# A selective-scan kernel on one core: the scan's operands trade memories, and GpSimd forms du*B for five states of sixteen

## The chip, the core and the metric

The kernel runs on one core of a Trainium2 chip. Its engines are named as the profile names them: PE is TensorE (matmuls), DVE is VectorE, ACT is ScalarE, POOL is GpSimd, SP is SyncE, which only issues transfers. The metric is device time in microseconds (us) of one execution; lower is better. Three executions of the kernel before took 4989.82, 4993.41 and 4997.49 us, and the median, 4993.41 us, is the time that the change is measured against.

## What is computed

Two layers follow each other. The change touches the first alone, a state-space block on a 4 x 48 x 48 x 128 image batch. Each image is projected to 256 channels, convolved, and read as a sequence of 2304 places in K = 4 directions. Each direction has N = 16 states per channel. For every state the first-order recurrence below runs along the sequence, and the 16 states are summed with the weights C:

```python
def step(h, inp):
    dt_l, u_l, B_l, C_l = inp
    dA = jnp.exp(dt_l[..., None] * A)
    h = h * dA + (dt_l * u_l)[..., None] * B_l[:, :, None, :]
    y = jnp.einsum('bkdn,bkn->bkd', h, C_l)
    return (h, y)
h0 = jnp.zeros((B, K, d, N), x.dtype)
_, ys = lax.scan(step, h0, (dt_t, u_t, B_t, C_t))
```

Around it stand a normalisation of the input, a softplus that makes dt, a normalisation and a gate behind the sum of the directions, and an output projection. The second layer is a Fourier neural operator with attention; it reads the first layer's output and stays as it is.

## The kernel before, in words

**Tiles and steps.** 256 channels lie as NF = 2 halves of 128 partitions. A sequence of 2304 places is cut into chunks of LC = 480 places (line 33), the last with 384. Four images, four directions and five chunks make 80 chunks; each has 16 steps, one for a state, so that there are 1280 steps. A step works on both halves at once: 2 x 480 elements per partition.

**What one step does.** The function names are those of lines 502 to 580.
- `fetch` (line 502) has SP load the rows of C for two states at a time, spread over all partitions, into `cbc` (three buffers); for a state that POOL drives it loads the row of B into `bbc` (two buffers).
- `drive_pool` (line 512) takes a buffer of `db` (three buffers, SBUF). For states with i % 4 == 3 (`POOLS`, line 604) POOL writes du*B into it.
- `spread` (line 519) has PE spread the row of B over the partitions into `pb`, one PSUM bank, for the other twelve states; `drive_in` (line 531) has DVE multiply du by `pb` into `db`.
- `decay` (line 538) has ACT write exp(dt*A) for both halves into `da`, one of two PSUM tiles of two banks each (line 478), chosen by i % 2. The first half ends at column 510, column 511 holds a zero that was set once (line 480), and the second half begins at 512. A last small ACT copy puts the state that was carried from the chunk before into the one column of `db` between the halves.
- `scan` (line 547) has DVE run one scan over 961 columns, h = da*h + db. At the parting column da is zero and db is the carried state, so the second half starts from its own state. The result goes to `h` (four buffers, SBUF).
- `read_out` (line 556) has POOL multiply `h` by C into `hc` (four buffers); `carry_on` (line 561) has ACT save the two last columns for the next chunk; `sum_up` (line 566) has PE add `hc` up in PSUM; `put_away` (line 582) has ACT copy the sums out after the sixteenth step.

**The order of the work** is written by hand. `LAGS` (line 626) lists the stages with how many steps behind the newest each runs, and `advance` (line 632) calls them in that order once for each new step. So on each engine the instructions stand in exactly this order (`Ordered`, line 36), while the transfers that SP issues may be placed earlier by the compiler. At the end of each round `piece` (line 610) emits one piece of side work: projections of the next direction (`project`, line 400), the next image's front part (`front`, line 260), an earlier chunk's output part (`back`, line 421). Side work waits its turn in the list `later`.

**Limits around it.** dt and the rows of B live in a ring of seven chunks (line 71); `project` may work on a chunk only once `done[0] + RING - 1` has reached its number (line 405), and its last piece runs the softplus of all five chunks of a direction (line 408). At step 11 of a direction's last chunk the rest of that projection is drained at once (line 694), since POOL then needs the first dt (`drive`, line 412).

Of the kernel before, what the change touches and what calls it, by code (L numbers as in the profile page):

```python
# [10 lines left out]
F32 = mybir.dt.float32  # L11
BF16 = mybir.dt.bfloat16
AF = mybir.ActivationFunctionType
# [10 lines left out]
NF = D // 128  # L24
N = 16
R = 8
K = 4
NX = 112
BANK = 512
NH = 32  # L30

LC = 480
CHUNKS = [(s, min(LC, L - s)) for s in range(0, L, LC)]


# [18 lines left out]
def first_layer(ctx, tc, io, x1_dram, sp_dram, d_w, d_m):  # L54
# [9 lines left out]
    on = Ordered(tc)  # L64
    const = ctx.enter_context(tc.tile_pool(name="l0_const", bufs=1))
    small = ctx.enter_context(tc.tile_pool(name="l0_small", bufs=2))
    one = ctx.enter_context(tc.tile_pool(name="l0_one", bufs=1))
    two = ctx.enter_context(tc.tile_pool(name="l0_two", bufs=2))
    three = ctx.enter_context(tc.tile_pool(name="l0_three", bufs=3))
    four = ctx.enter_context(tc.tile_pool(name="l0_four", bufs=4))  # L70
    ring = ctx.enter_context(tc.tile_pool(name="l0_ring", bufs=7))
    ps_a = ctx.enter_context(tc.tile_pool(name="l0_psa", bufs=1, space=PSUM))
    ps_s = ctx.enter_context(tc.tile_pool(name="l0_pss", bufs=1, space=PSUM))
    ps_b = ctx.enter_context(tc.tile_pool(name="l0_psb", bufs=1, space=PSUM))
# [24 lines left out]

    w_xp = const.tile([128, K, NF, NX], F32, name="w_xp")  # L100
    on.gpsimd.memset(w_xp, 0.0)
    w_x = const.tile([128, K, NF, R + 2 * N], F32, name="w_x")
    for k in range(K):
        nc.sync.dma_start(w_x[:, k], io["x_proj_wT"][k].rearrange("(f p) c -> p f c", p=128))
    for o, c0, c1 in ((0, R, R + 2 * N), (32, 0, R), (64, R, R + N), (96, R, R + N)):
# [258 lines left out]
    def project_chunk(c, w_dt, xc):  # L364


        k, s, n = c.k, c.s, c.n
        src = at(xc, k, s, n)
        px = side(f"px{c.t}")
        for f in range(NF):  # L370
            on.tensor.matmul(
                like(px[0:NX, 0:n], k), w_xp[:, k, f], src[:, f], start=(f == 0), stop=(f == NF - 1)
            )
            yield
        xd = two.tile([32 + R, LC], F32, tag="xd", name=f"xd{c.t}")
        on.scalar.copy(xd[:, 0:n], px[0 : 32 + R, 0:n])
        c.cd = dram.tile([2 * N, LC], F32, tag="cd", name=f"cd{c.t}")
        nc.sync.dma_start(c.cd[:, 0:n], xd[0 : 2 * N, 0:n])

        c.bs = ring.tile([NX, LC], BF16, tag="bs", name=f"bs{c.t}")  # L380
        on.scalar.copy(c.bs[:, 0:n], px[0:NX, 0:n])
        for q in range(2):
            on.tensor.matmul(px[0:NX, 0:n], less[:, q], c.bs[:, 0:n], start=False, stop=True, skip_group_check=True)
            yield
            rows = slice(64 + 32 * q, NX)
            on.scalar.copy(c.bs[rows, 0:n], px[rows, 0:n])
        c.dt = ring.tile([128, NF, LC], F32, tag="dt", name=f"dt{c.t}")
        for f in range(NF):
            pd = side(f"pd{c.t}_{f}")
            on.tensor.matmul(  # L390
                pd[:, 0:n],
                w_dt[32 : 32 + R, f * 128 : (f + 1) * 128],
                xd[32 : 32 + R, 0:n],
                start=True,
                stop=True,
            )
            yield
            on.scalar.activation(c.dt[:, f, 0:n], pd[:, 0:n], AF.Identity, bias=b_dt[:, k, f : f + 1])
# [77 lines left out]


    das = [ps_a.tile([128, 2 * BANK], F32, name=f"da{j}") for j in range(2)]
    for da in das:
        on.vector.memset(da[:, BANK - 1 : BANK], 0.0)  # L480
    carries = [const.tile([128, N, NF], F32, name=f"carry{j}") for j in range(2)]

    def halves(ap, n):

        return ap[:, 0 : 2 * (n + 1)].rearrange("p (f n) -> p f n", f=NF)[:, :, 0:n]

    class Chunk:


        def __init__(self, b, k, s, n, first, final, number, im):  # L490
            self.b, self.k, self.s, self.n, self.number, self.im = b, k, s, n, number, im
            self.first, self.final, self.rev = first, final, int(k >= 2)
            self.ready = False
            self.t = f"{b}_{k}_{s}"

    class Step:


        def __init__(self, c, i):
            self.c, self.i = c, i  # L500

    def fetch(u):
        c, i, n = u.c, u.i, u.c.n
        if i % NQ == 0:
            c.cbc = three.tile([128, NQ, LC], F32, tag="cbc", name=f"cbc{c.t}_{i}")
            nc.sync.dma_start(c.cbc[:, :, 0:n], c.cd[N + i : N + i + NQ, 0:n].partition_broadcast(128))
        u.cbc = c.cbc[:, i % NQ : i % NQ + 1, 0:n]
        if i % 4 == POOLS:
            u.bbc = two.tile([128, 1, LC], F32, tag="bbc", name=f"bbc{c.t}_{i}")
            nc.sync.dma_start(u.bbc[:, :, 0:n], c.cd[i : i + 1, 0:n].partition_broadcast(128))  # L510

    def drive_pool(u):

        c, i, n = u.c, u.i, u.c.n
        u.db = three.tile([128, NF * (LC + 1)], F32, tag="db", name=f"db{c.t}_{i}")
        if i % 4 == POOLS:
            on.gpsimd.tensor_mul(halves(u.db, n), c.du[:, :, 0:n], u.bbc[:, :, 0:n].to_broadcast([128, NF, n]))

    def spread(u):

        c, i, n = u.c, u.i, u.c.n
        if i == N - 1:
            done[0] = c.number + 1
        if i % 4 == POOLS:
            return
        u.pb = ps_b.tile([128, 512], F32, tag="pb", name=f"pb{c.t}_{i}")
        on.tensor.matmul(
            u.pb[:, 0:n], pick[:, i : i + 1].to_broadcast([NX, 128]), c.bs[:, 0:n], start=True, stop=True
        )

    def drive_in(u):
        c, i, n = u.c, u.i, u.c.n
        if i % 4 != POOLS:
            on.vector.tensor_mul(
                halves(u.db, n), c.du[:, :, 0:n], u.pb[:, None, 0:n].to_broadcast([128, NF, n])
            )

    def decay(u):
        c, i, n = u.c, u.i, u.c.n
        u.da = das[i % 2]  # L540
        for f in range(NF):
            q = c.k * NF + f
            o = BANK if f else BANK - 1 - n
            on.scalar.activation(u.da[:, o : o + n], c.dt[:, f, 0:n], AF.Exp, scale=a_neg[:, q, i : i + 1])
        on.scalar.copy(u.db[:, n : n + 1], c.carry[:, i, 1 - c.rev : 2 - c.rev])

    def scan(u):
        c, i, n = u.c, u.i, u.c.n
        u.h = four.tile([128, NF * (LC + 1)], F32, tag="h", name=f"h{c.t}_{i}")
        m = 2 * n + 1  # L550
        ha, aa, ba = u.h[:, 0:m], u.da[:, BANK - 1 - n : BANK + n], u.db[:, 0:m]
        if c.rev:
            ha, aa, ba = ha[:, ::-1], aa[:, ::-1], ba[:, ::-1]
        on.vector.tensor_tensor_scan(ha, aa, ba, c.carry[:, i, c.rev : c.rev + 1], ALU.mult, ALU.add)
# [45 lines left out]


    ORDER = (0, 2, 1, 3)
    RING = 7
    POOLS = 3
    WAIT, FREE = object(), object()
    current = [None]
    done = [0]
# [13 lines left out]
    def drain(gen):  # L621
        while gen in later:
            piece()


    LAGS = (
        (0, fetch), (9, put_away), (2, drive_pool), (4, drive_in), (5, scan), (4, decay), (6, carry_on),
        (5, read_out), (3, spread), (8, sum_up),
    )
    window = deque([None] * 10, 10)  # L630

    def advance(u):
        window.appendleft(u)
        for lag, stage in LAGS:
            if window[lag] is not None:
                stage(window[lag])
        piece()
# [30 lines left out]
    for j, chunks in enumerate(directions):  # L668
# [9 lines left out]
        for m, c in enumerate(chunks):  # L678
            c.carry = carries[j % 2]
            for i in range(N):  # L680
# [6 lines left out]
                if i in (N // 2 + 3, N // 2 + 6):  # L687
# [5 lines left out]
                    elif nxt is not None:  # L693
                        drain(nxt)
                        drive(directions[j + 1][0], f)
                advance(Step(c, i))
                if not chunks[-1].ready and not j:
                    piece()
    for _ in range(len(window)):
# [1287 lines left out]
```

## Time and profile before

| What | Value |
|---|---|
| median of three executions | 4993.41 us (4989.82 to 4997.49) |
| profiled execution, first to last instruction (span) | 4987.4 us |
| DVE busy over the span | 4169.9 us (84%) |
| POOL busy over the span | 3992.7 us (80%) |
| PE, ACT busy over the span | 4176.6 us, 2964.0 us |
| first and last scan begin at | 76.8 us, 4176.0 us |
| DMA share of 16 engines, mean | 32.5% on SP's queue |

The profile describes one execution of its own, whose only time is its span: it leaves out what lies before the first and after the last instruction. The shortest of the three timed executions is 2.4 us longer than that span, the median 6.0 us. A row of the groups gives an engine, an operation, what is written and read, how often it runs, its total busy time and the mean of one, and then the engine's idle time just before it with what ended that idle time. Each row mixes shapes unless they are kept apart. A wait is put down to what came last, so the name behind the arrow is the last missing thing, not always the cause.

### The profile page before, as it was taken

The numbers are of one execution on the slowest core, as the hardware profiler recorded it, in microseconds if no ns is written. First come the engines' busy times: TensorE is split into PE (matmuls) and PEld (weight loads), VectorE is DVE, ScalarE is ACT, GpSimd is POOL, SyncE is SP. The second block draws the span as 40 slices with busy tenths as digits, with TensorE's granted clock in tenths as the row PEclk, the third lists the DMA queues.
The fourth block names the chain that finished last, engine by engine and source line by source line (L and its number), as shares of the span: only waits on it lengthen the run. The fifth ranks groups of instructions, "written<-read, shape, count | busy, mean of one in ns | idle before, by whom it ended". The sixth has DMA issues, their size and how long they took to land.

```text
span 4987.4 us, 44228 instructions
## 1 busy us (share of the span) xinstructions
PE 4176.6 (84%) x12444; PEld 1913.7 (38%) x12444; DVE 4169.9 (84%) x2901; ACT 2964.0 (59%) x6608; POOL 3992.7 (80%) x2188
## 2 busy tenths in 40 slices
PE   6888898888798998887989888877888786879876
PEld 3334433333343333333433333333333432445443
DVE  3599998989899989898999998888999985557636
ACT  3566566666666666766666676665767654323344
POOL 4589998989899989888999998888999985146631
PEclk9989999999899999998999999998999988989977
DMA  1223232323232333232323233233333322236636
GB/s 55 74 87 100 94 113 91 104 85 102 90 107 94 116 95 99 89 100 92 104 95 115 93 98 94 98 104 92 104 107 102 105 92 90 48 71 147 146 101 151
DMA packets 276388, 491.57 MB, mean 99 GB/s; under 512 B 105685, under 2 KB 189781, under 8 KB 275565
## 3 DMA queue, kind: packets, MB, share of 16 engines
q1 hardware_dynamic: 270560, 485.67, 32.5%
q10 hardware_dynamic: 5580, 3.08, 0.3%
q8 instruction: 98, 1.61, 0.1%
q14 instruction: 150, 1.22, 0.1%
HBM read 453.49 MB, written 35.38 MB: 98 GB/s over the span
## 4 chain that ended last, share of the span: by engine, by line
DVE 18%; PE 15%; issue 7%; ACT 7%; POOL 3%; DMA 2%; SPq 1%; DVEq 0%; POOLq 0%; ACTq 0%
DVE h L50 12%; PE yp L50 4%; ACT da L50 3%; DVE db L50 3%; PE acc L1404 2%; ACT L50 1%; PE sc L1267 1%; POOL v L1400 1%; POOL db L50 1%; PE pi_p L50 1%; DMA xrep<-dxt 1%; ACT dt L50 1%; POOL hc L50 1%; ACT ws L50 1%; PE px L50 1%
## 5 line engine op out<-in xcount | busy, mean ns | idle before, releaser
L50 POOL TENSOR_TENSOR hc<-h,cbc 128x960 f32<-128x960 f32 (+1 forms) x1280 | 2718.7, 2140 | 448.3 <-DVE h L50 335.8
L50 DVE TENSOR_TENSOR_SCAN h<-da,carry,db 128x961 f32<-128x961 f32 (+1 forms) x1280 | 2701.8, 2129 | 164.9 <-ACT carry L50 107.1
L50 ACT ACTIVATE da<-dt,a_neg 128x480 f32<-128x480 f32 (+1 forms) x2560 | 1666.6, 651 | 1176.6 <-DVE h L50 1130.8
L50 PE MATMUL yp<-hc,ident 128*128 128x480 f32 (+1 forms) x5120 | 2277.5, 572 | 17.7 <-POOL hc L50 17.4
L50 PEld LDWEIGHTS yp<-hc,ident 128*128 128x128 f32 x5120 | 1005.6, 198 | 1381.0 <-issue 1006.0
L50 DVE TENSOR_TENSOR db<-du,pb 128x960 f32<-128x960 f32 (+1 forms) x960 | 1063.8, 1108 | 233.2 <-PE pb L50 177.8
L50 POOL TENSOR_TENSOR db<-du,bbc 128x960 f32<-128x960 f32 (+1 forms) x320 | 688.9, 2153 | 17.2 <-DMA d_m<-in_wK 8.5
L50 PE MATMUL pb<-bs,pick 112*128 112x480 bf16 (+1 forms) x960 | 358.0, 373 | 351.9 <-DVE db L50 350.0
L50 PE MATMUL pc<-pad,cdiag 128*128 128x480 f32 (+1 forms) x630 | 284.1, 563 | 6.6 <-ACT pad L50 6.6
L1400 POOL TENSOR_TENSOR v<-grep,xrep 128x768 f32<-128x768 f32 x96 | 174.9, 1823 | 87.3 <-PE acc L1404 48.7
L50 ACT COPY db<-carry 128x1 f32<-128x1 f32 x1280 | 228.5, 178 | 19.5 <-POOL db L50 13.5
L1404 PE MATMUL acc<-v,attn_c 128*64 128x384 f32 x1152 | 211.5, 504 | 26.7 <-DVE v L1396 13.6
L50 POOL TENSOR_TENSOR du<-dt,xc 128x480 f32<-128x480 f32 (+1 forms) x160 | 204.9, 1281 | 34.0 <-ACT dt L50 34.0
L1396 DVE TENSOR_TENSOR v<-gp,xrep 128x1536 f32<-128x1536 f32 x96 | 168.0, 1756 | 74.4 <-PE acc L1404 46.4
L50 PE MATMUL px<-xc,w_xp 128*112 128x480 f32 (+1 forms) x320 | 214.0, 756 | 17.1 <-ACT xc L50 13.3
L50 PEld LDWEIGHTS <-pick 112*128 112x128 bf16 x960 | 97.7, 102 | 329.4 <-issue 306.1
L50 ACT ACT_TABLE_LOAD x148 | 189.9, 1283 | 50.3 <-DMA ws_M<-in_wM1s 26.7
L50 PE MATMUL pd<-xd,w_dt 8*128 8x480 f32 (+1 forms) x320 | 168.0, 605 | 40.0 <-ACT bs L50 24.5
L50 ACT COPY carry<-h 128x2 f32<-128x2 f32 x1024 | 194.4, 190 | 0.0
L50 PEld LDWEIGHTS pc<-pad,cdiag 128*128 128x128 f32 x630 | 122.1, 194 | 139.4 <-issue 114.6
L50 PE MATMUL yp<-y,ident 128*128 128x480 f32 (+1 forms) x240 | 166.3, 823 | 0.2
L1404 PEld LDWEIGHTS acc<-v,attn_c 128*64 128x64 f32 x1152 | 119.2, 139 | 108.5 <-issue 53.7
(366 smaller groups left out, 3102.2 us busy)
## 6 DMA issues: line engine op xcount, KB each, us to landing
cbc<-cd SPq DMA_DIRECT2D x512, 480.0 KB
bbc<-cd SPq DMA_DIRECT2D x256, 240.0 KB
cbc<-cd SPq DMA_DIRECT2D x128, 384.0 KB
xrep<-dxt SPq DMA_DIRECT2D x48, 576.0 KB
bbc<-cd SPq DMA_DIRECT2D x64, 192.0 KB
grep<-dgt SPq DMA_DIRECT2D x16, 576.0 KB
x<-in_xT SPq DMA_DIRECT2D x16, 288.0 KB
xr<-in_xT SPq DMA_DIRECT2D x16, 288.0 KB
```

Source lines behind the costliest of these rows:

```text
L50: return lambda *args, **kw: self._tc.keep_in_program_order(emit(*args, **kw))
L1267: nc.tensor.matmul(sc[64 * b : 64 * b + 64, g, 0 : 8 * T], qs[:, j, n, 2 * pair + b], f[b][:, 8 * g : 8 * g + 8], start=(jn == 0), stop=False,
L1396: nc.vector.tensor_mul(v, gp[:, None, :, 0:NC].to_broadcast([128, 2, 2, NC]), x[:, :, 0:2])
L1400: nc.gpsimd.tensor_mul(v3, r[:, 2:3].to_broadcast([128, 2, NC]), x[:, :, 2])
L1404: nc.tensor.matmul(acc[c][64 * b : 64 * b + 64, 0:NC], attn_c[:, 2 * pair + b, g, q], v[:, b, c] if c < 2 else v3[:, b], start=first, stop ...
```

## The change

The sixteen states get kinds by the string `KINDS`: eleven V (DVE forms du*B) and five P (POOL does, for i = 2, 5, 8, 11, 14; before there were four, i = 3, 7, 11, 15).
- **V states.** The decay no longer goes to PSUM but to one of three SBUF tiles, `ahead`, chosen by the running step number modulo 3, and ACT writes it one round earlier (lag 3 in place of 4). DVE now writes du*B into the PSUM tile `held`, which is what `da` was, and the scan reads decay from SBUF and du*B from PSUM.
- **P states** keep decay in PSUM (`held`) and du*B in SBUF (`db`, now two buffers), at lag 4 as before.
- **Two parting columns** in place of one: halves stand at columns 482 apart in `h` and `db`, scans run over 962 columns. `part` has ACT write them: for a V state the carried state into two columns of `held`; for a P state the carried state into `db`, and zeros into `held` where a V state used it last. All five P states of a chunk follow a V state on the same tile. The decay tiles' own zeros are set once.
- **Room.** The ring of dt and B rows goes from seven chunks to six; `xd` has one buffer in place of two; a start-up tile, `w_x`, shares the place of `y`.

```diff
@@ -30,6 +30,10 @@
 NH = 32
 LC = 480
+GAP = 2
+AHEAD = 3
+RING = 6
+KINDS = "VVPVVPVVPVVPVVPV"
 CHUNKS = [(s, min(LC, L - s)) for s in range(0, L, LC)]
@@ -68,7 +72,7 @@
     two = ctx.enter_context(tc.tile_pool(name="l0_two", bufs=2))
     three = ctx.enter_context(tc.tile_pool(name="l0_three", bufs=3))
     four = ctx.enter_context(tc.tile_pool(name="l0_four", bufs=4))
-    ring = ctx.enter_context(tc.tile_pool(name="l0_ring", bufs=7))
+    ring = ctx.enter_context(tc.tile_pool(name="l0_ring", bufs=RING))
     ps_a = ctx.enter_context(tc.tile_pool(name="l0_psa", bufs=1, space=PSUM))
     ps_s = ctx.enter_context(tc.tile_pool(name="l0_pss", bufs=1, space=PSUM))
     ps_b = ctx.enter_context(tc.tile_pool(name="l0_psb", bufs=1, space=PSUM))
@@ -99,7 +103,7 @@
     w_xp = const.tile([128, K, NF, NX], F32, name="w_xp")
     on.gpsimd.memset(w_xp, 0.0)
-    w_x = const.tile([128, K, NF, R + 2 * N], F32, name="w_x")
+    w_x = one.tile([128, K, NF, R + 2 * N], F32, tag="y", name="w_x")
     for k in range(K):
         nc.sync.dma_start(w_x[:, k], io["x_proj_wT"][k].rearrange("(f p) c -> p f c", p=128))
     for o, c0, c1 in ((0, R, R + 2 * N), (32, 0, R), (64, R, R + N), (96, R, R + N)):
@@ -372,7 +376,7 @@
                 like(px[0:NX, 0:n], k), w_xp[:, k, f], src[:, f], start=(f == 0), stop=(f == NF - 1)
             )
             yield
-        xd = two.tile([32 + R, LC], F32, tag="xd", name=f"xd{c.t}")
+        xd = one.tile([32 + R, LC], F32, tag="xd", name=f"xd{c.t}")
         on.scalar.copy(xd[:, 0:n], px[0 : 32 + R, 0:n])
         c.cd = dram.tile([2 * N, LC], F32, tag="cd", name=f"cd{c.t}")
         nc.sync.dma_start(c.cd[:, 0:n], xd[0 : 2 * N, 0:n])
@@ -476,13 +480,17 @@
     das = [ps_a.tile([128, 2 * BANK], F32, name=f"da{j}") for j in range(2)]
-    for da in das:
-        on.vector.memset(da[:, BANK - 1 : BANK], 0.0)
+    parted = [True, True]
+    zero = const.tile([128, GAP], F32, name="zero")
+    on.gpsimd.memset(zero, 0.0)
+    ahead = [const.tile([128, 2 * LC + GAP], F32, name=f"ahead{j}") for j in range(AHEAD)]
+    for t in ahead:
+        on.gpsimd.memset(t[:, LC : LC + GAP], 0.0)
     carries = [const.tile([128, N, NF], F32, name=f"carry{j}") for j in range(2)]
     def halves(ap, n):
-        return ap[:, 0 : 2 * (n + 1)].rearrange("p (f n) -> p f n", f=NF)[:, :, 0:n]
+        return ap[:, 0 : 2 * (n + GAP)].rearrange("p (f n) -> p f n", f=NF)[:, :, 0:n]
     class Chunk:
@@ -496,8 +504,9 @@
     class Step:
-        def __init__(self, c, i):
-            self.c, self.i = c, i
+        def __init__(self, c, i, g):
+            self.c, self.i, self.g, self.kind = c, i, g, KINDS[i]
+            self.held = das[i % 2]
     def fetch(u):
         c, i, n = u.c, u.i, u.c.n
@@ -505,15 +514,15 @@
             c.cbc = three.tile([128, NQ, LC], F32, tag="cbc", name=f"cbc{c.t}_{i}")
             nc.sync.dma_start(c.cbc[:, :, 0:n], c.cd[N + i : N + i + NQ, 0:n].partition_broadcast(128))
         u.cbc = c.cbc[:, i % NQ : i % NQ + 1, 0:n]
-        if i % 4 == POOLS:
+        if u.kind == "P":
             u.bbc = two.tile([128, 1, LC], F32, tag="bbc", name=f"bbc{c.t}_{i}")
             nc.sync.dma_start(u.bbc[:, :, 0:n], c.cd[i : i + 1, 0:n].partition_broadcast(128))
     def drive_pool(u):
-        c, i, n = u.c, u.i, u.c.n
-        u.db = three.tile([128, NF * (LC + 1)], F32, tag="db", name=f"db{c.t}_{i}")
-        if i % 4 == POOLS:
+        c, n = u.c, u.c.n
+        if u.kind == "P":
+            u.db = two.tile([128, NF * (LC + GAP)], F32, tag="db", name=f"db{c.t}_{u.i}")
             on.gpsimd.tensor_mul(halves(u.db, n), c.du[:, :, 0:n], u.bbc[:, :, 0:n].to_broadcast([128, NF, n]))
     def spread(u):
@@ -521,34 +530,60 @@
         c, i, n = u.c, u.i, u.c.n
         if i == N - 1:
             done[0] = c.number + 1
-        if i % 4 == POOLS:
+        if u.kind != "V":
             return
         u.pb = ps_b.tile([128, 512], F32, tag="pb", name=f"pb{c.t}_{i}")
         on.tensor.matmul(
             u.pb[:, 0:n], pick[:, i : i + 1].to_broadcast([NX, 128]), c.bs[:, 0:n], start=True, stop=True
         )
+    def half(ap, m, f, n):
+        o = m + GAP if f else m - n
+        return ap[:, o : o + n]
+    def whole(ap, m, n):
+        return ap[:, m - n : m + GAP + n]
+    IN_PS = BANK - GAP
     def drive_in(u):
+        c, n = u.c, u.c.n
+        if u.kind == "V":
+            on.vector.tensor_mul(
+                halves(u.held[:, IN_PS - n :], n), c.du[:, :, 0:n], u.pb[:, None, 0:n].to_broadcast([128, NF, n])
+            )
+    def decay(u, kind):
         c, i, n = u.c, u.i, u.c.n
-        if i % 4 != POOLS:
-            on.vector.tensor_mul(
-                halves(u.db, n), c.du[:, :, 0:n], u.pb[:, None, 0:n].to_broadcast([128, NF, n])
-            )
-    def decay(u):
-        c, i, n = u.c, u.i, u.c.n
-        u.da = das[i % 2]
+        if u.kind != kind:
+            return
+        u.da, m = (u.held, IN_PS) if kind == "P" else (ahead[u.g % AHEAD], LC)
         for f in range(NF):
             q = c.k * NF + f
-            o = BANK if f else BANK - 1 - n
-            on.scalar.activation(u.da[:, o : o + n], c.dt[:, f, 0:n], AF.Exp, scale=a_neg[:, q, i : i + 1])
-        on.scalar.copy(u.db[:, n : n + 1], c.carry[:, i, 1 - c.rev : 2 - c.rev])
+            on.scalar.activation(half(u.da, m, f, n), c.dt[:, f, 0:n], AF.Exp, scale=a_neg[:, q, i : i + 1])
+        u.da = whole(u.da, m, n)
+    def part(u):
+        c, i, n = u.c, u.i, u.c.n
+        start = c.carry[:, i, 1 - c.rev : 2 - c.rev].to_broadcast([128, GAP])
+        between = u.held[:, IN_PS:BANK]
+        if u.kind == "P":
+            if parted[i % 2]:
+                on.scalar.copy(between, zero)
+            on.scalar.copy(u.db[:, n : n + GAP], start)
+            u.db = u.db[:, 0 : 2 * n + GAP]
+        else:
+            on.scalar.copy(between, start)
+            u.db = whole(u.held, IN_PS, n)
+        parted[i % 2] = u.kind != "P"
     def scan(u):
         c, i, n = u.c, u.i, u.c.n
-        u.h = four.tile([128, NF * (LC + 1)], F32, tag="h", name=f"h{c.t}_{i}")
-        m = 2 * n + 1
-        ha, aa, ba = u.h[:, 0:m], u.da[:, BANK - 1 - n : BANK + n], u.db[:, 0:m]
+        u.h = four.tile([128, NF * (LC + GAP)], F32, tag="h", name=f"h{c.t}_{i}")
+        ha, aa, ba = u.h[:, 0 : 2 * n + GAP], u.da, u.db
         if c.rev:
             ha, aa, ba = ha[:, ::-1], aa[:, ::-1], ba[:, ::-1]
         on.vector.tensor_tensor_scan(ha, aa, ba, c.carry[:, i, c.rev : c.rev + 1], ALU.mult, ALU.add)
@@ -600,8 +635,6 @@
     ORDER = (0, 2, 1, 3)
-    RING = 7
-    POOLS = 3
     WAIT, FREE = object(), object()
     current = [None]
     done = [0]
@@ -623,9 +656,10 @@
             piece()
+    decay_v, decay_p = partial(decay, kind="V"), partial(decay, kind="P")
     LAGS = (
-        (0, fetch), (9, put_away), (2, drive_pool), (4, drive_in), (5, scan), (4, decay), (6, carry_on),
-        (5, read_out), (3, spread), (8, sum_up),
+        (0, fetch), (9, put_away), (2, drive_pool), (4, drive_in), (5, scan), (3, decay_v), (4, decay_p),
+        (4, part), (6, carry_on), (5, read_out), (3, spread), (8, sum_up),
     )
     window = deque([None] * 10, 10)
@@ -693,7 +727,7 @@
                     elif nxt is not None:
                         drain(nxt)
                         drive(directions[j + 1][0], f)
-                advance(Step(c, i))
+                advance(Step(c, i, c.number * N + i))
                 if not chunks[-1].ready and not j:
                     piece()
     for _ in range(len(window)):
```

## The prediction, made before the result was known

> **What bounds the kernel now.** I read the page's busy table and its slices first: DVE and POOL are both at nine tenths or more from 250 to 4200 us, the scan's stage, so the next view is the table of groups, shapes kept apart.
>
> ```profile
> L50 POOL TENSOR_TENSOR hc<-h,cbc 128x960 f32<-128x960 f32 x1024 | 2259.1, 2220 | 404.0 <-DVE h L50 306.7 <-issue 45.8 <-PE yp L50 21.4
> L50 DVE TENSOR_TENSOR_SCAN h<-da,carry,db 128x961 f32<-128x961 f32 x1024 | 2244.0, 2209 | 130.5 <-ACT carry L50 107.1 <-POOL hc L50 19.5 <-ACT db L50 3.9
> L50 DVE TENSOR_TENSOR db<-du,pb 128x960 f32<-128x960 f32 x768 | 881.7, 1148 | 210.4 <-PE pb L50 166.8 <-DVE h L50 2.8
> L50 POOL TENSOR_TENSOR db<-du,bbc 128x960 f32<-128x960 f32 x256 | 571.7, 2233 | 0.0
> ```
>
> A state costs DVE a 2.21 us scan and, twelve times in sixteen, a 1.15 us multiply; it costs POOL a 2.22 us multiply and, four times in sixteen, another. Which of the two is late? The table of waits says POOL waits for the scan far more than the scan for POOL (19.5 us):
>
> ```profile
> ACT da L50 <- DVE h L50: 1130.8, 874, 5.9
> POOL hc L50 <- DVE h L50: 335.8, 273, 14.3
> DVE db L50 <- PE pb L50: 177.8, 115, 46.5
> DVE h L50 <- ACT carry L50: 107.1, 35, 4.8
> DVE h L50 <- ACT db L50: 38.2, 11, 8.3
> ```
>
> So DVE sets the pace, POOL is close behind, and DVE's own stops are PE's spread row and a late ACT. The timeline of DVE, start and length of each piece, gives the pace to a hundredth:
>
> ```profile
> 3773.24 1.16 DVE L50 TENSOR_TENSOR db<-du,pb 128x960 f32<-128x960 f32 x1
> 3774.32 2.22 DVE L50 TENSOR_TENSOR_SCAN h<-da,carry,db 128x961 f32<-128x961 f32 x1
> 3776.64 1.16 DVE L50 TENSOR_TENSOR db<-du,pb 128x960 f32<-128x960 f32 x1
> 3777.71 4.32 DVE L50 TENSOR_TENSOR_SCAN h<-da,carry,db 128x961 f32<-128x961 f32 x2
> 3781.94 1.13 DVE L50 TENSOR_TENSOR db<-du,pb 128x960 f32<-128x960 f32 x1
> 3782.99 2.22 DVE L50 TENSOR_TENSOR_SCAN h<-da,carry,db 128x961 f32<-128x961 f32 x1
> 3785.31 1.16 DVE L50 TENSOR_TENSOR db<-du,pb 128x960 f32<-128x960 f32 x1
> 3786.38 2.22 DVE L50 TENSOR_TENSOR_SCAN h<-da,carry,db 128x961 f32<-128x961 f32 x1
> ```
>
> Four steps take 3786.38 - 3774.32 = 12.06 us, 48.24 a chunk. Multiply to scan is 1.07, scan to scan 2.12. A multiply follows a scan either after 2.10 (3781.94, overlapping its end) or after 2.32 (3776.64, 0.10 after its end). I read the second as a wait for that scan to end, since it must free a buffer. Two stretches of the same view by windows, each one chunk, show the two regimes:
>
> ```profile
> 1501.70:1549.90 48.20, 45.21 (x111) 19.25 (x110) 47.37 (x29) 29.66 (x74) 46.07 (x23) 1.00 0.32 104
> 1800.00:1853.70 53.70, 46.12 (x108) 19.63 (x108) 47.14 (x29) 36.59 (x81) 45.88 (x23) 0.97 0.28 88
> ```
>
> The third and fifth busy figures are DVE and POOL. The plain chunk has DVE full; in the second, ACT runs a burst (softplus of five chunks, between two table loads, some 7 us) and both engines stand still. Cut so, the 80 chunks add up to 4101 us with 389 us of DVE idle and 453 of POOL idle.
>
> **What the Trainium skill says.** "GPSIMD Engine Reference", section 3.1, puts a two-input multiply on GpSimd at about 2.6 cycles of 1.2 GHz an element: 2.08 us for 960 and a start; the trace's 2.22 agrees. "SBUF — State Buffer", "Who interferes with whom", says a DVE instruction with one SBUF input does not contend with GpSimd. The trace agrees: scans, with one operand in each memory, stay at 2.21 us (median and longest). The change keeps one operand in each, so I charge no contention. "PSUM — Partial Sum Buffer", on bank collisions, says accesses of two engines to one bank must be ordered; here this bears on `part`, whose ACT copy goes into the bank that DVE's multiply fills. No trace of before shows that pair. "Perfetto Trace Analysis", "Optimizing Scalar/DVE Operations", gives DVE about 60 ns of access on SBUF and 125 on PSUM; no large DVE write to PSUM is in this trace.
>
> **The change, part by part**, against the profiled span, 4987.4 us.
>
> *DVE's pace.* 80 multiplies go (one a chunk). But a multiply for V now writes the tile that the scan two steps earlier has just read, and in the order multiply(s), scan(s-1) that scan is always the instruction ahead of it. So I expect every V step to be of the 2.32 sort: eleven steps of 2.32 + 1.07 = 3.39 and five of 2.12, 47.9 us a chunk against 48.24. That is 0.35 x 77 (64 full chunks and 16 of four fifths) = 27 us less.
>
> *POOL's load.* 80 multiplies come: 64 x 2.18 + 16 x 1.79 (their pitch at 960 and 768) = 168 us. A plain chunk's POOL goes from 46.1 to 48.2: now it is POOL that is full. Chunk by chunk I set POOL's busy time plus its added multiply against the stretch less 0.35: in 27 of 80 it is larger, by 29 us together (2.5 at most, where POOL had no idle time). In the others POOL's idle time hides it. With both engines at 48, small delays that one had swallowed for the other no longer vanish; I put 0.3 us on each of the other 53, 16 us, by choice. The 80 more loads of `bbc` are hidden: SP issues them several steps ahead and the DMA engines are a third busy.
>
> *PE's spread row.* `pb` has one buffer, so a row is made between two multiplies. Where one scan alone lies between them it is tight: eight pairs a chunk before, five or six in V V P. Of the 178 us waited, 46.5 is one event; of the other 132, a third could go, 40; I take 25 less.
>
> *ACT, one step earlier.* A V decay can start when scan(s-3) has ended, not scan(s-2). But `part` for s cannot: it writes the tile of scan(s-2), behind multiply(s), and in ACT's order it stands behind decay of s+1, itself waiting for scan(s-2). So ACT gets no further ahead than before. The decays (0.67 us each) also bunch up: the round before a P state has none, the P round has two pairs and two copies. From scan(s-2)'s end that is 4 x 0.66 + 2 x 0.18 = 3.0 us and some 0.1 to start, while DVE needs it after a scan, a multiply and a late start, 2.12 + 1.07 + 0.1 = 3.3. Before, ACT had 1.5 us to do in that time. Queued behind a late `part` are the carry copies and side work; the scan waits, and POOL behind it. In plain chunks it just fits. A piece of side work left over from the round before (0.55 to 0.66 us, a table load 1.28) makes the scan late. Bounds: nothing, and 0.4 us at 400 P states, 160 us. I take 20. The zero copies, 400 x 0.18, lie in ACT's idle time; if that is gone, they are in this bound.
>
> *Ring of six.* A direction's last projection may now start only after the fourth chunk ends: round 2 of the fifth. It has seven pieces, then the softplus, and must be done by round 11, else it is drained at once while POOL waits for dt. Side work of the front that holds its turn makes it late. The burst moves to where ACT is bunched, too. Bounds 0 and 15 directions x 4 us; I take 20. `xd`'s one buffer is covered by the pieces between two projections.
>
> *DVE writing PSUM.* The page's difference, 65 ns, on 880 multiplies is 57 us as an estimate; the other end is -20, if writes there end sooner. I take 10. The extra column is 2.3 ns x 1280 = 3 us.
>
> Sum: -27 + 29 + 16 - 25 + 20 + 20 + 10 + 3 = +46: a span of 5033, and with the 6 us from span to median, 5040.
>
> **Rivals.** *Faster: the scan no longer waits for the exponentials.* If what was late of ACT was the pair of decays and not the copy behind them, the early decays take off half of the 145 us of ACT waits. With pace, spread row, POOL, columns and no ring or bunching cost: -27 - 25 + 29 + 16 - 72 + 10 + 3 = -66, 4927. It decides from the point where `part` is ready before the scan ahead has ended even after side work. Against it speaks `part`'s place in ACT's queue; for it, the many stops of 2 to 4 us. *ACT bound at P states:* 0.3 us at each of 400 is 120 in place of 20, about 5140; for it speaks ACT's 31 to 40 us busy a chunk in the heavy stretches. *It cancels:* POOL's added work falls into stops that remain, ring and bunching cost nothing, about 4994; then the change does not do what it says, since the decay ahead is held back by `part`.
>
> **How the numbers follow.** The forecast, POOL and DVE level with small losses, has a chance of 0.50 and its own range of 5004 to 5090; faster 0.18; ACT bound 0.20; cancelling 0.12. Within 0.2% (10 us) counts as the same, about what a measurement of this kernel can tell. The range runs from 4935 to 5130: it takes in the upper half of the faster case and the lower of the ACT-bound one.
>
> **What would show it.** Right: POOL idle time before `hc` falls by over 100 us, plain chunks stay near 48.2, multiplies after scans start at 2.3, DVE waits for ACT grow. Wrong: multiplies start at 2.1; ACT waits under 100 us; a DVE multiply well over 1.2 us; the softplus burst hidden by POOL's backlog, which would be the faster case.

## The result, and the profile after

The changed kernel takes 5127.78 us (median of 4 runs, 5122.42 to 5130.61) against 4995.45 us for the kernel before beside it: a ratio of 1.0266 with a 95% interval of 1.0251 to 1.0280. It is slower, by 132 us; the forecast was 46 us slower. The profiled execution has a span of 5128.8 us, 141 us more than before's 4987.4. Below, a difference of ratios of 0.01 is 50 us.

First the groups of the scan stage, shapes kept apart (busy us, mean ns of one | idle time of the engine ahead of it, and what ended it):

```profile
L54 POOL TENSOR_TENSOR hc<-h,cbc 128x960 f32<-128x960 f32 x1024 | 2097.6, 2057 | 446.2 <-PE yp L54 170.7 <-DVE h L54 133.6 <-issue 77.9
L54 DVE TENSOR_TENSOR_SCAN h<-ahead,carry,da 128x962 f32<-128x962 f32 x704 | 1526.8, 2204 | 40.8 <-ACT da L54 36.5 <-POOL du L54 3.9 <-POOL db L54 0.4
L54 DVE TENSOR_TENSOR da<-du,pb 128x960 f32<-128x960 f32 x704 | 818.2, 1162 | 321.1 <-PE pb L54 263.7 <-DVE h L54 1.4 <-PE yp L54 0.5
L54 POOL TENSOR_TENSOR db<-du,bbc 128x960 f32<-128x960 f32 x320 | 711.3, 2223 | 11.5 <-DMA bbc<-cd 8.1 <-DMA d_m<-in_wQ 2.7 <-ACT da L54 0.6
L54 DVE TENSOR_TENSOR_SCAN h<-da,carry,db 128x962 f32<-128x962 f32 x320 | 709.2, 2216 | 63.0 <-ACT db L54 59.4 <-POOL hc L54 2.0 <-ACT carry L54 0.8
```

On VectorE and GpSimd no operation became slow. The scan is where it was (2204 and 2216 ns, before 2209), and VectorE's multiply into PSUM takes 1162 ns, before 1148. GpSimd's read-out multiply `hc` has even become shorter, 2057 ns against 2220. What grew is idle time: 321 us ahead of VectorE's multiply (before 210) and, the shorter chunks included, 566 us ahead of `hc` (before 448). The table of waits (total us, times, longest) says for whom:

```profile
ACT da L54 <- DVE da L54: 809.2, 409, 4.1
ACT ahead L54 <- DVE h L54: 423.0, 309, 2.3
DVE da L54 <- PE pb L54: 315.6, 147, 49.3
POOL hc L54 <- PE yp L54: 215.4, 142, 5.5
POOL hc L54 <- DVE h L54: 174.2, 141, 14.1
DVE h L54 <- ACT db L54: 107.0, 44, 7.9
DVE h L54 <- ACT da L54: 77.9, 29, 13.9
PE pd L54 <- ACT bs L54: 76.7, 37, 9.2
```

VectorE waits for the spread row `pb` 138 us longer than before (177.8), and for ScalarE 40 us longer (184.9 against 145.3). GpSimd waits 189 us longer for TensorE to empty `hc` (before 26.2). Some of that comes with the fifth P state alone: in e5 below, which is quicker than the kernel before, GpSimd waits 108.4 us there. TensorE itself waits 76.7 us for ScalarE's cast `bs` at the projection `pd` (before 24.5). So the new waits point through TensorE to ScalarE.

TensorE has also become slower at work that the change does not touch, the summing of `hc` into `yp`. Its rows before, in the changed kernel, and in e10 below, which runs the changed kernel's instructions in the same order but takes 101 us less:

```profile
L50 PE MATMUL yp<-hc,ident 128*128 128x480 f32 (+1 forms) x5120 | 2277.5, 572 | 17.7 <-POOL hc L50 17.4
L54 PE MATMUL yp<-hc,ident 128*128 128x480 f32 (+1 forms) x5120 | 2364.5, 591 | 17.3 <-POOL hc L54 17.1
L54 PE MATMUL yp<-hc,ident 128*128 128x480 f32 (+1 forms) x5120 | 2319.4, 581 | 29.4 <-POOL hc L54 29.2
```

The clock that TensorE was granted, averaged over the span, is 0.931, 0.907 and 0.925 of full speed in these three profiles. The clock records of these traces know only full and half speed. In the changed kernel 518 of the 5120 matmuls began at half speed (286 before, 398 in e10); they took 912 ns on average, the others 554. The lower clock goes with the kernel: it is 0.906 to 0.908 in the four executions of the changed kernel, and 0.923 to 0.925 in those of e10.

In an undisturbed stretch the pace is what was forecast. VectorE's timeline:

```profile
1481.81 4.32 DVE L54 TENSOR_TENSOR_SCAN h<-ahead,carry,da 128x962 f32<-128x962 f32 x2
1486.23 1.16 DVE L54 TENSOR_TENSOR da<-du,pb 128x960 f32<-128x960 f32 x1
1487.31 2.22 DVE L54 TENSOR_TENSOR_SCAN h<-da,carry,db 128x962 f32<-128x962 f32 x1
1489.62 1.16 DVE L54 TENSOR_TENSOR da<-du,pb 128x960 f32<-128x960 f32 x1
1490.70 4.32 DVE L54 TENSOR_TENSOR_SCAN h<-ahead,carry,da 128x962 f32<-128x962 f32 x2
```

Three steps (V, V, P) take 1490.70 - 1481.81 = 8.89 us; forecast were 2 x 3.39 + 2.12 = 8.90. A plain chunk takes 47.8 us (48.2 before). Added up from one chunk's first scan to the next one's, the 80 chunks take 4228.1 us against 4101.4. Plain chunks did not get longer, so the loss, 127 us, is in the chunks in which ScalarE and TensorE also have side work.

### The profile page after: what moved, and what is told of

It reads as the page before. It is cut to its first block, busy times and chain, and to the rows that moved or that the text cites. A ratio compares the mean times of both kernels' runs of the same rounds, so it can differ in the third digit from the quotient of the medians.

```text
span 5128.8 us, 44987 instructions
## 1 busy us (share of the span) xinstructions
PE 4280.9 (83%) x12364; PEld 1944.3 (38%) x12364; DVE 4113.9 (80%) x2819; ACT 2934.3 (57%) x7006; POOL 3970.6 (77%) x2272
## 4 chain that ended last, share of the span: by engine, by line
PE 34%; DVE 29%; issue 14%; ACT 14%; POOL 5%; DMA 3%; SPq 0%; DVEq 0%; ACTq 0%; POOLq 0%
DVE h L54 22%; PE yp L54 16%; DVE da L54 4%; ACT ahead L54 3%; ACT da L54 3%; PE pd L54 3%; PE pc L54 3%; ACT L54 2%; ACT dt L54 1%; PE pb L54 1%; POOL hc L54 1%; PE px L54 1%; POOL v L1434 1%; PE acc L1438 1%; DMA xrep<-dxt 1%
## 5 line engine op out<-in xcount | busy, mean ns | idle before, releaser
L54 POOL TENSOR_TENSOR hc<-h,cbc 128x960 f32<-128x960 f32 (+1 forms) x1280 | 2525.5, 1982 | 566.1 <-PE yp L54 215.4
L54 PE MATMUL yp<-hc,ident 128*128 128x480 f32 (+1 forms) x5120 | 2364.5, 591 | 17.3 <-POOL hc L54 17.1
L54 DVE TENSOR_TENSOR_SCAN h<-ahead,carry,da 128x962 f32<-128x962 f32 (+1 forms) x880 | 1839.0, 2124 | 84.7 <-ACT da L54 77.9
L54 PEld LDWEIGHTS yp<-hc,ident 128*128 128x128 f32 x5120 | 1037.8, 204 | 1410.9 <-issue 1106.4
L54 ACT ACTIVATE ahead<-dt,a_neg 128x480 f32<-128x480 f32 (+1 forms) x1760 | 1097.5, 671 | 426.0 <-DVE h L54 423.0
L54 DVE TENSOR_TENSOR da<-du,pb 128x960 f32<-128x960 f32 (+1 forms) x880 | 987.7, 1122 | 387.9 <-PE pb L54 315.6
L54 DVE TENSOR_TENSOR_SCAN h<-da,carry,db 128x962 f32<-128x962 f32 (+1 forms) x400 | 854.5, 2136 | 110.6 <-ACT db L54 107.0
L54 POOL TENSOR_TENSOR db<-du,bbc 128x960 f32<-128x960 f32 (+1 forms) x400 | 856.3, 2141 | 20.3 <-DMA bbc<-cd 16.9
L54 ACT COPY da<-carry 128x2 f32<-128x2 f32 x880 | 141.4, 161 | 810.9 <-DVE da L54 809.2
L54 ACT ACTIVATE da<-dt,a_neg 128x480 f32<-128x480 f32 (+1 forms) x800 | 511.0, 639 | 13.0
L54 PE MATMUL pd<-xd,w_dt 8*128 8x480 f32 (+1 forms) x320 | 195.3, 695 | 85.0 <-ACT bs L54 76.7
```

The lines of the kernel that those rows point to most:

```text
L54: return lambda *args, **kw: self._tc.keep_in_program_order(emit(*args, **kw))
```

## The experiments

**The parts alone.** Three kernels start from the kernel before.

*e1: the ring of six alone* (before; `l0_ring` bufs and `RING` from 7 to 6).

> The kernel before with one edit, the ring of dt and B rows cut from seven chunks to six. Ring theory (the late last projection, drained with the softplus at the end of each direction, is what the change lost): +80 to +140 us over before, most of the 132 us, with softplus bursts in the fifth chunk. Parting-copy theory (ACT's copy waits on DVE's multiply and on bunched decays at every P state): +0 to +40 us.

Measured: 5008.2 us, ratio 1.0039 (1.0024 to 1.0054). That is 20 us. The softplus bursts moved into the fifth chunk of a direction, as in the changed kernel, so the ring does move them, but that is not the bulk of the loss.

*e3: the two parting columns alone.*

```
-        return ap[:, 0 : 2 * (n + 1)].rearrange("p (f n) -> p f n", f=NF)[:, :, 0:n]
+        return ap[:, 0 : 2 * (n + 2)].rearrange("p (f n) -> p f n", f=NF)[:, :, 0:n]
...
-            o = BANK if f else BANK - 1 - n
+            o = BANK if f else BANK - 2 - n
```

> The kernel before with two parting columns in place of one and nothing else. If the even start of the second half is what made POOL's read-out 2.06 us in place of 2.22, the read-out shows 2.06 here as well, POOL's busy time falls by about 190 us, and since DVE sets the pace the time moves little: -40 to 0 us. If the read-out got shorter because the V scans' operands changed place, it stays at 2.22 and the time at before's.

Measured: 4980.09 us, 0.9983 (0.9976 to 0.9990). The group of its read-out:

```profile
L50 POOL TENSOR_TENSOR hc<-h,cbc 128x960 f32<-128x960 f32 x1024 | 2101.5, 2057 | 548.5 <-DVE h L50 402.2 <-issue 53.4 <-PE yp L50 29.2
```

2057 ns, as in the changed kernel, with nothing else altered: the second column is what shortens `hc`. Its idle time grows in step, for VectorE sets the pace here, so only some 8 us of it are seen.

*e5: the columns and the fifth P state, operands not exchanged* (e3 with `KINDS = "VVPVVPVVPVVPVVPV"` in place of `i % 4 == POOLS`).

> The kernel before with two parting columns and the five P states of the change (i = 2, 5, 8, 11, 14), operands left where they were: decay in PSUM, du*B in SBUF, ring of seven. ACT-blocking theory (in the change ACT stands at the parting copy until DVE's multiply has ended, its side work comes late, PE waits for that in order, and the spread row for the next multiply is late): the swap of operands is what costs, so this is at before or under it, 4920 to 4990, DVE waits for the spread row at 80 us or less. If the fifth P state is what costs (POOL too full): 5050 to 5130.

Measured: 4947.48 us, 0.9917 (0.9903 to 0.9932), faster than both kernels. The fifth P state is worth 0.0066, 33 us.

**The buffers of the changed kernel.**

*e2: a ring of seven* (changed kernel, `RING = 7`, one buffer of `bbc` for the room).

> The kernel after with a ring of seven again; one of the two bbc buffers is given up for the room. Ring theory: 80 to 140 us come back, 4990 to 5050. Parting-copy theory: 5090 to 5130, ACT waits stay. If the single bbc buffer hurts, POOL shows idle time before its du*B multiplies that ends with a DMA.

Measured: 5126.12 us, 1.0280 (1.0262 to 1.0297): nothing comes back.

*e8: two buffers of `xd`* (changed kernel).

> The kernel after with two buffers for xd again. If xd's one buffer is what makes PE wait for ACT in the projections (PE's waits for bs rose from about 25 to 77 us), 30 to 80 us come back. ACT-blocking theory: within 10 us of after.

Measured: 5126.5 us, 1.0270 (1.0248 to 1.0292): nothing.

**The place of the early decay.** Six kernels change the place or the tiles of ScalarE's work in the changed kernel, and little else. What comes back is given by the ratios, since the kernel before was measured anew beside each group of runs.

*e4: the parting copy first.*

```
-        (0, fetch), (9, put_away), (2, drive_pool), (4, drive_in), (5, scan), (3, decay_v), (4, decay_p),
-        (4, part), (6, carry_on), (5, read_out), (3, spread), (8, sum_up),
+        (0, fetch), (9, put_away), (2, drive_pool), (4, drive_in), (5, scan), (4, decay_p), (4, part),
+        (3, decay_v), (6, carry_on), (5, read_out), (3, spread), (8, sum_up),
```

> The kernel after with the parting copies ahead of the V decays in the order of each round (decay of P, parting copies, then decay of V one step ahead). Parting-copy theory: the scan's waits for ACT (185 us) fall by half or more, -50 to -100 us. Ring theory: within 30 us of after, since the burst and the drained projection stay.

Measured: 5090.28 us, 1.0213 (1.0188 to 1.0237): 27 us of the 133 come back.

*e6: the parting copy a round later, just ahead of its scan* (`(5, part), (5, scan)`, and no `(4, part)`), so that ScalarE seldom stands at it.

> The kernel after with the parting copies one round later, just ahead of the scan in the order, so that DVE's multiply has ended long before and ACT does not stand still for it; side work of the round comes before the copy. ACT-blocking theory: ACT's waits for the DVE multiply (809 us) all but vanish, DVE's waits for the spread row fall from 316 us towards 180, time 5010 to 5070. If ACT standing at the copy is harmless, it stays at 5090 to 5130, or gets worse as the copies now come late for the scan.

Measured: 5166.47 us, 1.0356 (1.0340 to 1.0371), worse. ScalarE's waits at the copy did fall, from 809.2 to 334.5 us, but the table of waits of this run shows what took their place:

```profile
ACT ahead L54 <- DVE h L54: 590.6, 363, 2.5
...
ACT da L54 <- DVE da L54: 334.5, 280, 5.7
ACT carry L54 <- DVE h L54: 279.2, 232, 2.0
...
DVE h L54 <- ACT da L54: 218.3, 95, 16.4
```

The scan now waits 218.3 us for its copy, and ScalarE stands as long as before, only elsewhere (590.6 + 334.5 + 279.2 = 1204 us, against 809.2 + 423.0 = 1232). So this run alone does not say whether standing at the copy costs. e10 below does: there ScalarE stands at the copy for 1022 us, longer than in the changed kernel, and the time falls.

*e7: the decay of V states in the round of before* (`(4, decay_v)` in place of `(3, decay_v)`).

> The kernel after with V decays at the lag of before, in the round of their own parting copy, so that no round has two pairs of decays. If the bunching at P states is what costs, the waits of P scans for ACT (107 us) fall under 40 and 40 to 80 us come back. ACT-blocking theory: ACT still stands at each multiply, so at most 40 us.

Measured: 5015.91 us, 1.0058 (1.0041 to 1.0075): 104 us of the 133 come back from one digit. VectorE's wait for `pb` is 189.0 us again.

*e9: still one round ahead, but behind the round's piece of side work.*

```
         for lag, stage in LAGS:
             if window[lag] is not None:
                 stage(window[lag])
         piece()
+        if window[3] is not None:
+            decay_v(window[3])
```

(with `(3, decay_v)` taken out of `LAGS`, and `(4, decay_p)`, `(4, part)` where they were).

> The changed kernel with the early decay of a V state moved behind the round's piece of side work in ScalarE's order (the decay is still one round ahead; the same instructions are issued). Theory A, bunching: in the round of a P state ScalarE has two pairs of exponentials ahead of its side work, and TensorE, in order, stands at the late side work and makes the spread row late; then most of the 112 us that the decay one round later gave comes back: 5015 to 5050, and VectorE's wait for `pb` falls from 206 us (250 to 4170 us) to about 100. Rival B: having the decay early is itself what costs (its tile's traffic, or ScalarE standing at the decay's wait for the scan three steps earlier, wherever it is queued): 5110 to 5140. If only ScalarE's urgent work for the scan matters (the P pair and the parting copy), and not the side work, about 5090, as when the parting copy went first.

Measured: 5035.4 us, 1.0098 (1.0083 to 1.0113): 84 us come back. By its round the decay is as early as in the changed kernel, but in ScalarE's own queue this is nearly the order of e7: in the two traces about a tenth of the decays stand elsewhere, and nothing on TensorE, VectorE or GpSimd. So e9 repeats e7 more than it adds to it. Behind the copies alone (e4) 27 us came back, behind the side work too (e7, e9) 104 and 84: what the decay must not stand ahead of is the side work.

*e10: a fourth tile for the early decay* (`AHEAD = 4`, one buffer of `bbc`; order as in the changed kernel).

> The changed kernel with four tiles for the early decays in place of three (one buffer of `bbc` in place of two makes the room), so that a decay waits for the scan four steps earlier. If ScalarE's standing at the decay (423 us of waits for the scan) holds up the work queued behind it, 5020 to 5080 and that wait nearly gone. If the cost is the bunched work itself and not the wait, 5115 to 5140, as changed.

Measured: 5016.63 us, 1.0064 (1.0047 to 1.0081): 101 us come back, about as much as in e7. The rows of its table of waits that answer to those above:

```profile
ACT da L54 <- DVE da L54: 1022.1, 557, 4.5
ACT da L54 <- DVE h L54: 90.0, 171, 1.1
...
DVE da L54 <- PE pb L54: 215.0, 130, 49.3
POOL hc L54 <- DVE h L54: 156.5, 126, 14.2
POOL hc L54 <- PE yp L54: 145.4, 125, 5.0
...
PE pd L54 <- ACT bs L54: 45.3, 37, 7.9
```

ScalarE hardly waits for scans now (90 us, at the decays of P states, against 423), though it stands longer at the parting copy. VectorE's wait for `pb`, GpSimd's for `yp` and TensorE's for `bs` all fall back, by 101, 70 and 31 us. The compute instructions and their order on every engine are those of the changed kernel, but for one memset at the start; what differs is the scan that releases the decay, and the one buffer of `bbc`, which costs nothing in e15 below. The same place in the two timelines (start, length, engine, what; in brackets the wait). First the changed kernel, from the scan of a direction's second chunk:

```profile
1989.95 4.32 DVE L54 TENSOR_TENSOR_SCAN h<-ahead,carry,da 128x962 f32<-128x962 f32 x2
...
1992.20 1.28 ACT L54 ACTIVATE ahead<-dt,a_neg 128x480 f32<-128x480 f32 x2 [1.20 <-DVE h L54]
1993.39 1.34 ACT L54 ACTIVATE da<-dt,a_neg 128x480 f32<-128x480 f32 x2
...
1995.16 0.55 ACT L54 CAST bs<-px 16x480 bf16<-16x480 f32 x1
...
1995.77 1.07 PE L54 MATMUL pd<-xd,w_dt 8*128 8x480 f32 x2 [2.86 <-ACT bs L54]
...
1996.98 2.29 PE L54 MATMUL yp<-hc,ident 128*128 128x384 f32 x4
...
2006.11 0.37 PE L54 MATMUL pb<-bs,pick 112*128 112x480 bf16 x1
2006.51 1.16 DVE L54 TENSOR_TENSOR da<-du,pb 128x960 f32<-128x960 f32 x1 [3.35 <-PE pb L54]
```

And with the fourth tile:

```profile
1949.21 4.32 DVE L54 TENSOR_TENSOR_SCAN h<-ahead,carry,da 128x962 f32<-128x962 f32 x2
...
1950.29 1.28 ACT L54 ACTIVATE ahead<-dt,a_neg 128x480 f32<-128x480 f32 x2
...
1951.47 1.35 ACT L54 ACTIVATE da<-dt,a_neg 128x480 f32<-128x480 f32 x2
1953.26 0.55 ACT L54 CAST bs<-px 16x480 bf16<-16x480 f32 x1
...
1953.86 1.07 PE L54 MATMUL pd<-xd,w_dt 8*128 8x480 f32 x2 [1.69 <-ACT bs L54]
...
1955.07 1.46 PE L54 MATMUL yp<-hc,ident 128*128 128x384 f32 x4
...
1963.69 0.37 PE L54 MATMUL pb<-bs,pick 112*128 112x480 bf16 x1
1964.09 1.16 DVE L54 TENSOR_TENSOR da<-du,pb 128x960 f32<-128x960 f32 x1 [1.67 <-PE pb L54]
```

Count from the scan's start. In the changed kernel ScalarE stands 1.20 us at the early decay until the first of the two scans has ended (2.25 us); then come two pairs of exponentials, and the cast of the projection is 5.21 us after the scan's start. With the fourth tile the decay starts at 1.08 and the cast is at 4.05, 1.16 us earlier. TensorE, in order, stands at `pd` for that cast 2.86 us in one and 1.69 in the other, and everything queued behind `pd` is late with it. Then the clock adds to it: in the changed kernel it is at half speed from 1997.46 to 2004.28 us, with the fourth tile only from 1960.03 to 1963.44, and the four `yp` matmuls behind `pd` take 2.29 us in place of 1.46. A few steps on, the spread row is at 16.16 against 14.48 us, 1.68 later, and VectorE stands 3.35 us against 1.67. This is one place, shown as an example.

*e13: standing without the double pair* (e7 with `AHEAD = 2`).

> The changed kernel with the V decay in the same round as before (as in the run that gave 5016) and with two tiles for it in place of three: where the state two steps earlier was a V state, the decay must wait for the scan that ended last, as in the changed kernel, but no round has two pairs of exponentials in ScalarE's queue. If standing at the decay alone costs, 5080 to 5130. If the cost comes from standing and the double pair together, 5010 to 5040.

Measured: 5018.21 us, 1.0053 (1.0033 to 1.0074), no worse than e7. And ScalarE does stand at its decays:

```profile
ACT da L54 <- DVE h L54: 421.8, 320, 1.9
...
ACT ahead L54 <- DVE h L54: 153.8, 231, 1.9
```

Of these 576 us of waiting for scans, 422 stand in e7 too (423.5), and the 154 added cost nothing that can be seen. 423 us in the changed kernel cost some 100. Standing alone is not the price. It costs where two pairs of exponentials and the copies lie behind the same scan, ahead of side work. Nor is the double pair alone the price: e10 has it, and is as quick as e7. How much of the price is TensorE's lateness in its queue, and how much the slower clock that comes with it, no run here separates.

**What is left beside the early decay.**

*e11: no early decay and a ring of seven* (e7 with `RING = 7`, one buffer of `bbc`).

> The changed kernel with the V decay in the same round as before and with the ring of seven (one buffer of `bbc` makes the room): what is left is the exchange of operands with the two columns and the fifth P state. If the parts add up, 5016 less the ring's 20: 4996, some 48 above the kernel with two columns and five P states alone (4947). If the ring costs only beside the lag of before, or `bbc`'s one buffer costs, 5010 to 5030. If the exchange costs nothing once the rest is as before, 4945 to 4960.

Measured: 4972.09 us, 0.9968 (0.9955 to 0.9980), 25 us above e5. e2 differs from this kernel in the early decay alone, at 1.0280: with a ring of seven the early decay costs 156 us, with the ring of six 104.

*e14: the ring of six in e5.*

> The kernel with two columns and five P states, operands not exchanged (4947), with a ring of six. If the ring costs the same everywhere, 20 us: 4967. If it costs more once the chunks are shorter and the fifth P state leaves GpSimd less idle time, 44 as between the two runs with exchanged operands: 4990. In that case the ring and the fifth P state are the pair that interacts, not the ring and the exchange.

Measured: 4974.84 us, 0.9968 (0.9960 to 0.9977): 25 us above e5, about as in the kernel before (20), less than from e11 to e7 (45).

*e15: one buffer each of `bbc` and `xd` in e5.*

> The kernel with two columns and five P states, operands not exchanged (4947), with one buffer each for bbc and xd. If the 25 us left beside the exchange come from a late load of bbc or a late xd, 4960 to 4972; if they come from the exchange itself (ScalarE's parting copy behind VectorE's multiply, the write to PSUM), 4945 to 4952.

Measured: 4948.15 us, 0.9914 (0.9893 to 0.9935): nothing. So the 25 us between e5 and e11 belong to the exchange with what it brings along: the copies, and two buffers of `db` in place of three.

*e12: six P states without the exchange* (e5 with `KINDS = "VVPVVPVPVVPVVPVP"`).

> The kernel before with two parting columns and six P states a chunk (positions 2, 5, 7, 10, 13, 15), operands not exchanged. By the paces of VectorE (3.31 us a V step, 2.12 a P step) a plain chunk falls from 47.0 to 45.8 us, GpSimd's work is 16 x 2.02 + 6 x 2.18 = 45.4. If VectorE still sets the pace: up to 92 us less than 4947, half of it in the chunks with side work, so 4890 to 4930. If GpSimd, now level, or side work sets it: 4940 to 4970.

Measured: 4924.68 us, 0.9877 (0.9861 to 0.9892), the fastest of all, 63 us below the kernel before beside it. At the pitch of before, 2.18 us for each of its multiplies, GpSimd would need 22 x 2.18 = 48 us a chunk, more than the 45.8 expected of VectorE. So by this estimate it has the room for the sixth only because its read-out is shorter; that was not tried.

## Why the prediction was wrong

The sign was right, the size was not, and most of the loss came by a road that the prediction had not priced. The measured 5127.78 us lies at the upper end of its outer range, 4935 to 5130, far from the 5040 forecast. Put one after the other, the parts are (ratios of the runs above, in us by 5000):

| step | ratio after it | us | the prediction's term |
|---|---|---|---|
| two parting columns (e3) | 0.9983 | -8 | +3 |
| fifth P state (e5) | 0.9917 | -33 | pace -27, GpSimd +29 and +16 |
| exchange of operands (e11) | 0.9968 | +25 | PSUM write +10, spread row -25 |
| ring of six (e7) | 1.0058 | +45 | +20 |
| decay one round ahead (changed) | 1.0266 | +104 | +20 |

Another order of the steps gives other numbers: with the early decay before the ring, the decay costs 156 us (e11 to e2) and the ring nothing (e2 to the changed kernel). Together the two are 149 us either way.

*ACT, one step earlier: the step that failed.* The prediction saw every piece of it: that the decay of the next step waits for the scan that had released the decay before, that ScalarE so gets no further ahead, that a P state's round has two pairs of exponentials, and that side work is queued behind. It then wrote "in plain chunks it just fits" and took 20 of a bound of 160.

The term is 104 us (e7 against the changed kernel; 101 by e10), and 156 with a ring of seven. In plain chunks it does fit, 47.8 us. What it priced was ScalarE's own lateness for the scan; that grew by only 40 us of waits over before, and by 11 over e7 (174.0). What it left out is the next reader of ScalarE's side work: TensorE stands in order at the projection for ScalarE's cast, with the spread row and the summing behind it, and its clock is lower too. Against e7, which differs in the early decay alone, VectorE waits 127 us longer for the spread row and GpSimd 90 us longer for the summing. That the early decay costs this, by its wait for the scan ahead of side work, is shown by e7 and e10; the road through TensorE is read from the tables of waits and one stretch of the timelines.

The rival with ScalarE as the bound at P states, 5140, had nearly the right time, but by luck: it took the direct way to the scan and not this one.

*POOL's load: wrong.* The added multiplies cost 711.3 + 145.0 - 571.7 - 117.1 = 167.5 us, as forecast (168). But the second column took 193.1 us off the read-out (2259.1 + 459.6 - 2097.6 - 428.0), more than was added, so GpSimd did not become full, and the fifth P state was a gain. The sign named for this, less idle time ahead of `hc`, did not show: it rose.

*DVE's pace: right in size, not in its reason.* The pace of 8.89 us in three steps is there. But in e5, where the multiply does not write the tile that a scan has just read, VectorE's timeline has the same multiply 2.32 us after a scan's start, and the same 8.89 us (3741.91 to 3750.80) for three steps:

```profile
3741.91 4.33 DVE L50 TENSOR_TENSOR_SCAN h<-da,carry,db 128x962 f32<-128x962 f32 x2
3746.34 1.16 DVE L50 TENSOR_TENSOR db<-du,pb 128x960 f32<-128x960 f32 x1
3747.41 2.21 DVE L50 TENSOR_TENSOR_SCAN h<-da,carry,db 128x962 f32<-128x962 f32 x1
3749.73 1.15 DVE L50 TENSOR_TENSOR db<-du,pb 128x960 f32<-128x960 f32 x1
3750.80 2.21 DVE L50 TENSOR_TENSOR_SCAN h<-da,carry,db 128x962 f32<-128x962 f32 x1
```

So the reason given, that the multiply writes the tile which a scan has just read, is not needed for the 2.32 us; what makes them was not found. The gain in pace comes from the fifth P state alone.

*PE's spread row: wrong.* No gain is seen even without the early decay (189.0 us of waits in e7, 193.7 in e11, 177.8 before).

*DVE writing PSUM: right.* 14 ns more at 960 elements and 15 at 768, on 880 multiplies: 12 us. The estimate from the Trainium skill's "Perfetto Trace Analysis", "Optimizing Scalar/DVE Operations", 65 ns each, was the far end of the range. The measured 12 us are half of the exchange's 25 us; where the rest lies (the zero copies, the parting copy behind VectorE's multiply, the two buffers of `db`) was not tried apart and stays open.

*Ring of six: right alone* (20 us in e1, 25 in e14), but 45 beside the exchange, and nothing in the changed kernel, where e2 gave none of it back. The terms do not add up freely; why the ring and the exchange together cost more is open.

## What to carry to other kernels

An instruction moved earlier in an in-order queue starts earlier only if its buffer is free earlier: ask which instruction releases it, and what is queued behind it when it isn't. Three tiles written one round ahead wait for a scan issued one round before, just as two tiles in the old round did. So nothing was gained, and the cast that another engine needed stood behind the wait; a fourth tile, or a place behind the side work, took the loss away. Price a late engine not at its direct reader alone but through each in-order queue that reads its side work, and look at TensorE's granted clock and its mean times in both profiles: a table of waits does not show that an engine has become slower.

## What the runs showed of the hardware

The time of GpSimd's two-input multiply depends on how its input is laid out. With one column between the two halves (the second begins at an odd fp32 column, 481) 960 elements take 2220 ns and 768 take 1818; with two columns (482) 2057 and 1682, in e3 with nothing else changed. The Trainium skill's "GPSIMD Engine Reference", section 3.1, as an estimate 2.08 us for 960, fits the even start; the prediction took the odd start's 2.22 for agreement. GpSimd's other multiply, `db<-du,bbc`, which writes the same layout and reads another, stays at 2225 ns in e3 (2233 before): the layout matters for this read, and was not seen to matter for that write. The second column moves both the start of the second half and its distance from the first; the two were not tried apart. VectorE's scan and multiply did not change with the second column (2211 against 2209 ns, 1147 against 1148).
